# The graph part of an expert layer's tail: gathers in small portions behind the experts' steps

## The chip, the cores and the metric

The kernel runs on one core of a Trainium2 chip. The metric is the device time of one execution in microseconds (us), the median of several runs. A profile is one more execution, taken by the hardware profiler.

## The reference, cut to what matters

The input is `x` of shape (4, 32, 96, 256), which is 12,288 tokens of 256 features. Layer 0 is a pair of Mamba scans over the two axes. Layer 1 is additive attention (`tanh` of all query and key pairs), and then an expert layer whose gates come from a graph attention. Only that last part is touched:

```python
h = (x_flat @ W_gat).reshape(M, HEADS, NUM_EXPERTS)          # 4 heads, 4 experts
a_src = (h * att_src).sum(-1);  a_dst = (h * att_dst).sum(-1)
e = leaky_relu(a_src[src] + a_dst[dst], negative_slope=0.2)   # random edges and one loop per token
ee = exp(e - e_max[dst]);  alpha = ee / segment_sum(ee, dst)[dst]
agg = segment_sum(h[src] * alpha, dst)
scores = layernorm(agg).reshape(M, HEADS, NUM_EXPERTS).mean(1)
topk_s, topk_i = top_k(scores, 2);  w = softmax(topk_s)
for ei in range(4):
    g = where(topk_i == ei, w, 0).sum(-1)
    out = out + g * (gelu(x @ W1[ei] + b1[ei]) @ W2[ei] + b2[ei])
```

The result is `out` plus the layer's input. The 1,048,576 edges have ends in a wider range than there are tokens. Indices beyond the tokens clip to the last one, so most edges are of a kind that is only counted; the rest, at most 108 columns of 128 edges for each quarter of the tokens, are gathered one by one.

## The kernel before, in words

Everything ahead of the tail is the same in both kernels. The tail (`tail()`, with the class `Graph` for the edges and the class `Experts`) does two things side by side, step by step, in one Python loop that lays out every engine's instructions in order.

**Experts.** There are 24 blocks of 512 tokens and 4 experts. A unit is one expert on one block, and takes 3 steps. 37 units are left for the tail: the last expert of blocks 6 to 16, two of block 17, and all four of blocks 18 to 23; the others were done earlier, beside the attention. A unit's hidden part is 16 matmuls `ph` (L1629) with Gelu on ScalarE (`h`, L1711); its output part, one unit later, is 32 matmuls `po` (L1637), with a bias added on VectorE (`ko`, L1701, or `o`, L1704). Where the gates of a block's quarter are not known yet when the block's turn comes, its outputs are kept: they are stored to DRAM (`kept`), and later, once the gates are there, loaded again (`all`, 2 MB) and added up with the gates onto the layer's input `y` (0.5 MB), 16 VectorE instructions (`y<-all,gates,y`, L1714) and a store of 0.5 MB to a block. Blocks 0 to 18 are kept, blocks 19 to 23 are gated at once (`y<-o,gates,y`).

**Edges.** A quarter's 108 columns are 9 portions of 12 columns (`GP`), called m in the loop. The quarters go in the order 3, 2, 0, 1. A portion passes through four operations:

- `gather`: 12 indirect DMAs `gs<-tab_s` (L1338), issued by GpSimd (POOL), bring the source rows; in quarter 3 alone 12 more, `gd<-tab_a` (L1045), bring the destination rows. The other quarters' `gd` were fetched during the attention. `gs` has four buffers.
- `scores`: five small VectorE instructions (L1352 to L1356), the exponential on ScalarE (L1282) and a product on VectorE (`v`, L1283).
- `spread`: for each of three groups of 4 columns (`GG`), VectorE makes one-hot tiles `ol` and `oh` (L1371) and the product `rh` (L1375).
- `place`: TensorE adds a group up into PSUM by 8 matmuls `pa` (L1385; 4 columns, two instructions each).

After a quarter's 9 portions `finish` makes its gates in five parts. `ready[q]` is the step from which a quarter's gates count as known.

In the tail's loop, what belongs to the edges stands in a list `todo` by steps: it is issued at the start of a step, ahead of that step's matmuls. Portion m has its scores at step 10 + 3m, its gathers all at once ten steps earlier, its three groups in the following steps, one to a step. So `ready` is 44, 71, 98 and 125, while the experts end at step 114. A kept block is due after its `ready`, at least 4 steps after the last such block; the loop runs to step 149.

The first own-edge line for each token (`own_edges`, L1303 to L1330) and `topa`, an all-reduce on POOL, are at the loop's start; the first portion's gathers are issued ahead of `topa`.

The kernel already has a pacing of another kind in the attention stage: there a gather is held back by a one-element copy on POOL (`mark<-th`, L689) of a value that ScalarE has just made.

Of the kernel before, what the change touches and what calls it, by code (L numbers as in the profile page):

```python
# [17 lines left out]
F32 = mybir.dt.float32  # L18
# [3 lines left out]
AF = mybir.ActivationFunctionType  # L22
ALU = mybir.AluOpType
# [3 lines left out]
P = 128  # L27
# [3 lines left out]
NT = TOK // P  # L31
# [18 lines left out]
JB = 512  # L50
# [9 lines left out]
G1, K1 = 8, 4  # L60
GP, GG = 12, 4
EDGE_US = 2.3
G0, PART = 10, 6
QUARTERS = 3, 2, 0, 1
KO_BUFS = 2
SLOT_US, PRODUCT_US = 1.2, 0.11
# [955 lines left out]
class Edges:  # L1022
# [19 lines left out]
    def gather(self, q, c):  # L1042
        if (q, c) not in self.have:
            self.have.add((q, c))
            self.nc.gpsimd.indirect_dma_start(  # L1045
                out=self.gd[:, q, c, :], out_offset=None,
                in_=self.tab_a[q].rearrange("p n f -> (p n) f"),
                in_offset=bass.IndirectOffsetOnAxis(ap=self.di[:, q, c:c + 1], axis=0))
# [203 lines left out]
class Graph:  # L1252
# [4 lines left out]
    def __init__(self, ctx, tc, a, ed, tab_s, tab_a, gates):  # L1257
        self.nc, self.ed = tc.nc, ed
        self.tab_s, self.tab_a, self.gates = tab_s, tab_a, gates
        pool = lambda name, bufs, **k: ctx.enter_context(tc.tile_pool(name=name, bufs=bufs, **k))  # L1260
        self.const, self.wk = pool("gc", 1), pool("gw", 2)
        self.ps = pool("gp", 2, space=PSUM)
        self.bg, self.lg, self.lb = (self.load(a, k, HF) for k in ("bg_rep", "lg_rep", "lb_rep"))
        self.eps = self.new("eps2", [P, 1])
        self.nc.vector.memset(self.eps, 1e-5)
        self.got, self.parts = {}, 4 * CQ // GP

    def new(self, name, shape):
        return self.const.tile(shape, F32, tag=name, name=name)
# [59 lines left out]
        nc.vector.tensor_tensor(wl, wl, ed.cnt.unsqueeze(2).to_broadcast([P, NH, ROW]), ALU.mult)  # L1329
        nc.vector.tensor_tensor(acc, acc, wl, ALU.add)  # L1330

    def gather(self, j):
        nc, ed = self.nc, self.ed
        gs = self.wk.tile([P, GP, ROW], F32, tag="gs", name="gs", bufs=4)
        q, c0 = divmod(j * GP, CQ)
        rows = self.tab_s.rearrange("p n f -> (p n) f")
        for u in range(GP):
            nc.gpsimd.indirect_dma_start(  # L1338
                out=gs[:, u, :], out_offset=None, in_=rows,
                in_offset=bass.IndirectOffsetOnAxis(ap=ed.si[:, q, c0 + u:c0 + u + 1], axis=0))  # L1340
            ed.gather(q, c0 + u)
        self.got[j] = gs

    def scores(self, j):
        nc = self.nc
        gs = self.got.pop(j)
        q, c0 = divmod(j * GP, CQ)
        gd = self.ed.gd[:, q, c0:c0 + GP, :]
        e = self.wk.tile([P, GP, HEADS], F32, tag="e", name="e")
        sh = self.wk.tile([P, GP, HEADS], F32, tag="sh", name="sh")  # L1350
        v = self.wk.tile([P, GP, ROW], F32, tag="v", name="v")
        nc.vector.tensor_tensor(e, gs[:, :, 0:HEADS], gd, ALU.add)  # L1352
        self.leaky(e)
        nc.vector.tensor_tensor(sh, gd, self.topa.unsqueeze(1).to_broadcast([P, GP, HEADS]), ALU.add)
        self.leaky(sh)
        nc.vector.tensor_tensor(e, e, sh, ALU.subtract)  # L1356
        self.weighted(e, v, gs[:, :, HEADS:], GP)
        self.v = v

    def spread(self, j, g):  # L1360

        nc, ed = self.nc, self.ed
        q, c0 = divmod(j * GP + g * GG, CQ)
        cols = slice(c0, c0 + GG)
        ol = self.wk.tile([P, GG, P], F32, tag="ol", name="ol")
        oh = self.wk.tile([P, GG, NT], F32, tag="oh", name="oh")
        rh = self.wk.tile([P, GG, NT, ROW], F32, tag="rh", name="rh")
        for to, among, which in ((ol, ed.lanes, ed.lane),
                                 (oh, ed.tiles[:, q * NT:(q + 1) * NT], ed.tile)):
            n = to.shape[2]  # L1370
            nc.vector.tensor_tensor(to, among.unsqueeze(1).to_broadcast([P, GG, n]),  # L1371
                                    which[:, q, cols].unsqueeze(2).to_broadcast([P, GG, n]),
                                    ALU.is_equal)
        v = self.v[:, g * GG:(g + 1) * GG, :]
        nc.vector.tensor_tensor(rh, oh.unsqueeze(3).to_broadcast([P, GG, NT, ROW]),  # L1375
                                v.unsqueeze(2).to_broadcast([P, GG, NT, ROW]), ALU.mult)
        return ol, rh

    def place(self, j, g, ol, rh):
        nc = self.nc  # L1380
        c0 = (j * GP + g * GG) % CQ
        if c0 == 0:
            self.pa = self.ps.tile([P, JB], F32, tag="pa", name="pa")
        for u in range(GG):
            nc.tensor.matmul(self.pa[:, :NT * ROW], ol[:, u, :],  # L1385
                             rh[:, u].rearrange("p n f -> p (n f)"),
                             start=(c0 + u == 0), stop=(c0 + u == CQ - 1))

    def finish(self, q):

        nc = self.nc
        cols = slice(q * NT, (q + 1) * NT)
        new = lambda name, shape: self.wk.tile(shape, F32, tag=name, name=name, bufs=1)
        acc, gates = self.acc[:, cols, :], self.gates[:, cols, :]
        nc.vector.tensor_tensor(acc, acc, self.pa[:, :NT * ROW].rearrange("p (n f) -> p n f", f=ROW),
                                ALU.add)
        yield from gates_of(nc, new, acc, gates, self.bg, self.lg, self.lb, self.eps)

# [328 lines left out]
def tail(tc, a, ed, ex, w, tab_s, tab_a, gates):  # L1727


    with ExitStack() as ctx:  # L1730
# [3 lines left out]
        units = [(i, e) for i in range(NBLK_X) for e in range(NEXP) if (i, e) not in ex.done]  # L1734
        todo = {}

        def at(t, f):
            todo.setdefault(t, []).append(f)

        own = gr.own_edges()  # L1740
        for n in range(3):
            at(2 * n, lambda: next(own, None))
        hot, ready = {}, {}
        PQ = CQ // GP
        for m in range(4 * PQ):
            j = QUARTERS[m // PQ] * PQ + m % PQ
            t = G0 + PART * m // 2
            if m < 1:
                gr.gather(j)
            else:  # L1750
                at(max(0, t - 10), lambda j=j: gr.gather(j))
            at(t, lambda j=j: gr.scores(j))
            for g in range(GP // GG):
                at(t + 1 + g, lambda j=j, g=g: hot.update({(j, g): gr.spread(j, g)}))
                at(t + 2 + g, lambda j=j, g=g: gr.place(j, g, *hot.pop((j, g))))
            if m % PQ == PQ - 1:
                fin, q = {}, QUARTERS[m // PQ]
                t += 2 + GP // GG
                at(t, lambda q=q, fin=fin: fin.update(g=gr.finish(q)))
                for n in range(5):  # L1760
                    at(t + n, lambda fin=fin: next(fin["g"], None))
                ready[q] = t + 5

        gr.tables()

# [5 lines left out]
        for i in sorted(kept, key=due.get):  # L1771
            v = {}

            def fetch(i=i, v=v):
                v["o"], v["y"] = ex.outputs_tile(), ex.sums(i, "y2")
                tc.nc.sync.dma_start(v["o"], ex.kept[i])

            def half(q0, i=i, v=v):
                for q in (q0, q0 + 1):
                    for e in range(NEXP):  # L1780
                        ex.add(i, e, q, v["y"], v["o"][:, q, e, :])
                if q0:
                    ex.store(i, v["y"])

            t = free = max(free + 4, due[i] + 1)
            at(t - 4, fetch)
            at(t, lambda half=half: half(0))
            at(t + 2, lambda half=half: half(2))

        to, hs = {}, {}  # L1790
        end = max(todo) + 1
        for t in range(max(3 * len(units) + 3, end)):
            n, part = divmod(t, 3)
            for f in todo.get(t, []):
                f()
            if n < len(units):
                i, e = units[n]
                if part == 0:
                    ex.fetch(i)
                    hs[n] = ex.hp.tile([P, FC, TB], F32, tag="h1", name="h1")  # L1800
                    if i in kept:
                        to[n] = ex.place()
                    else:
                        to[n] = ex.sums(i) if first[i] == n else to[n - 1]
                if part == 1 and n + 1 < len(units):
                    ex.fetch(units[n + 1][0])
                for f in ((0, 1), (2,), (3,))[part]:
                    ex.gelu(i, e, f, hs[n])
            if n and n - 1 < len(units) and part:
                i, e = units[n - 1]  # L1810
                ex.outputs(i, e, hs[n - 1], 2 * (part - 1), to[n - 1], i not in kept)
                if part == 2:
                    if i in kept:
                        ex.keep(i, e, to[n - 1])
                    elif last[i] == n - 1:
                        ex.store(i, to[n - 1])
# [267 lines left out]
```

## Time and profile before

| | us |
|---|---|
| Median of 3 runs | 15,269.78 (15,255.12 to 15,275.91) |
| Profiled execution | 15,342.51 |
| its span | 15,340.7, granted TensorE clock 0.891 |
| First expert matmul of the tail's loop | 14,239.9 |
| Last use of an expert's result (`y<-o`, L1714) | 15,229.8 |
| Last matmul | 15,258 |

The tail's work lies from about 14,200 us to the end of the span. In the page, "slices" are the span in 40 equal parts of 384 us with the busy tenths of each engine; PE is TensorE's matmul, PEld its weight loads, DVE VectorE, ACT ScalarE, POOL GpSimd. The "chain of waits" follows the work that ended last back from the end, each piece with its start and length. A "group" takes the instructions of one line and form together: busy us, mean ns of one, then the idle time of its engine just ahead of them, and what ended it. "Windows" give busy time and (in brackets) the number of instructions of each engine in a stretch.

### The profile page before, as it was taken

To read this page: it belongs to the slowest core of one execution; us is meant where nothing else is said; L and a number is where in the kernel's file an instruction comes from. 1 tells how busy PE (TensorE), PEld (TensorE's weight loads), DVE (VectorE), ACT (ScalarE), POOL (GpSimd) and SP (SyncE) were. 2 spreads that over 40 slices of the span, in tenths; PEclk is the share of its full clock that TensorE was granted. 3 is DMA by queue.
4 is the path that set the end of the run, shared out by engine and by line. 5 is a ranking of instruction groups with operands and counts; after the bars stand their busy time and mean duration, and the time that the engine had idled before them with its cause. 6 is when DMAs were issued, how large, how long until landed. Compare 5 with 4: busy or idle time off the path is not lost.

```text
span 15340.7 us, 224408 instructions
## 1 busy us (share of the span) xinstructions
PE 11721.4 (76%) x86496; PEld 5149.6 (34%) x86496; DVE 10713.9 (70%) x15462; ACT 12165.7 (79%) x9327; POOL 8797.1 (57%) x6727
## 2 busy tenths in 40 slices
PE   5666665777777767888887777788877888888797
PEld 2222232222222233333333333333333344433454
DVE  7888888777777887777777877577777733312368
ACT  3444334999999979999999899999997899999121
POOL 4655556777777767767777677477650144100663
PEclk8888887888888888899999889999988999999898
DMA  5666665445545454455554444355541000000223
GB/s 191 204 203 202 199 203 166 147 149 155 151 151 149 157 155 148 150 153 151 149 152 156 151 148 152 108 152 151 151 129 43 16 15 10 24 25 22 51 62 128
DMA packets 1197836, 1986.91 MB, mean 130 GB/s; under 512 B 411984, under 2 KB 645072, under 8 KB 1194320
## 3 DMA queue, kind: packets, MB, share of 16 engines
q1 hardware_dynamic: 1169104, 1967.10, 41.5%
q0 software_dynamic: 27648, 5.36, 0.7%
q8 instruction: 680, 11.14, 0.3%
q14 instruction: 404, 3.31, 0.1%
HBM read 1864.71 MB, written 107.35 MB: 129 GB/s over the span
## 4 chain that ended last, share of the span: by engine, by line
PE 23%; ACT 20%; DVE 7%; issue 4%; DMA 1%; POOL 1%; another core or an unknown queue 0%; SPq 0%; DVEq 0%; ACTq 0%; POOLq 0%
ACT th L823 14%; PE pe L796 9%; PE pv L902 3%; ACT dA L385 3%; PE pa L1385 2%; PE po L1637 2%; PE ph L1629 2%; DVE h L402 1%; ACT pr L886 1%; PE ptw L893 1%; PE ex L1554 1%; PE pz L459 1%; PE px L215 1%; DVE dB L393 1%
## 5 line engine op out<-in xcount | busy, mean ns | idle before, releaser
L823 ACT ACTIVATE th<-krep,qsel 128x3072 f32<-128x3072 f32 x3072 | 8666.9, 2847 | 380.4 <-PE pe L796 359.1
L796 PE MATMUL pe<-th,wa_blk 128*32 128x384 f32 x49152 | 5045.0, 539 | 1612.6 <-ACT pr L886 1382.7
L409 POOL TENSOR_TENSOR h<-h,bC 128x768 f32<-128x768 f32 x2048 | 3756.1, 1834 | 3012.2 <-DVE h L402 2638.5
L402 DVE TENSOR_TENSOR_SCAN h<-dA,dB 128x384 f32<-128x384 f32 x4096 | 3686.6, 941 | 1041.0 <-ACT dA L385 712.9
L796 PEld LDWEIGHTS pe<-th,wa_blk 128*32 128x32 f32 x49152 | 1458.9, 116 | 4171.2 <-issue 1967.3
L393 DVE TENSOR_TENSOR dB<-bB,dtu 128x768 f32<-128x768 f32 x2048 | 1942.3, 948 | 130.1 <-DMA bB<-bc 98.0
L385 ACT ACTIVATE dA<-dt,t_A 128x380 f32<-128x380 f32 x2048 | 1127.1, 571 | 897.9 <-DVE h L402 893.3
L385 ACT ACTIVATE dA<-dt,d_A 128x372 f32<-128x372 f32 x2048 | 1102.8, 562 | 606.0 <-DVE h L402 601.5
L428 PE MATMUL py<-h,ident 128*128 128x384 f32 x2176 | 990.7, 587 | 682.2 <-POOL h L409 681.3
L416 POOL TENSOR_TENSOR h<-h 128x768 f32<-128x768 f32 x752 | 1419.5, 1888 | 53.6
L902 PE MATMUL pv<-xn,pT 128*32 128x257 f32 x18432 | 1101.8, 387 | 131.4 <-DVE pT L895 130.8
L961 POOL TENSOR_SCALAR sf<-sel,f 128x32 f32<-128x32 f32 x384 | 146.0, 403 | 1584.0 <-ACT f L957 1480.9
L895 DVE COPY pT<-ptw 128x512 f32<-128x512 f32 (+1 forms) x768 | 419.3, 546 | 738.7 <-PE ptw L893 738.2
L428 PEld LDWEIGHTS py<-h,ident 128*128 128x128 f32 x2176 | 438.2, 219 | 1243.2 <-POOL h L409 1015.2
L418 POOL TENSOR_TENSOR y<-y,h 128x384 f32<-128x384 f32 x752 | 784.2, 1043 | 59.0
L902 PEld LDWEIGHTS pv<-xn,pT 128*32 128x32 f32 x18432 | 579.8, 111 | 707.7 <-DVE pT L895 257.0
L417 POOL TENSOR_TENSOR h<-h 128x384 f32<-128x384 f32 x752 | 782.0, 1040 | 59.0
L1338 POOL DMA_INDIRECT gs<-tab_s,si x432 | 496.6, 1149 | 324.7 <-DVE v L1283 171.2
L879 DVE TENSOR_REDUCE nb<-pe 128x1 f32<-128x768 f32 x384 | 362.2, 943 | 408.7 <-PE pe L796 408.6
L1711 ACT ACTIVATE h<-ph,b 128x512 f32<-128x512 f32 x148 | 101.2, 687 | 688.6 <-PE ph L1629 513.5
L904 DVE COPY pvs<-pv 128x257 f32<-128x257 f32 x384 | 160.6, 418 | 609.7 <-PE pv L902 608.2
L893 PE MATMUL ptw<-ident,pr 128*128 128x128 f32 x2304 | 475.5, 324 | 106.6 <-DVE pT L895 37.6
(276 smaller groups left out, 14969.7 us busy)
## 6 DMA issues: line engine op xcount, KB each, us to landing
bB<-bc SPq DMA_DIRECT2D x2048, 384.0 KB
bC<-bc SPq DMA_DIRECT2D x2048, 384.0 KB
all<-kept SPq DMA_DIRECT2D x19, 2048.0 KB
x<-x SPq DMA_DIRECT2D x144, 256.0 KB
x<-x SPq DMA_DIRECT2D x192, 128.0 KB
xt<-xn2T SPq DMA_DIRECT2D x41, 512.0 KB
kept<-ko SPq DMA_DIRECT2D x39, 512.0 KB
qsel<-xn2T SPq DMA_DIRECT2D x75, 256.0 KB
```

The lines of the kernel that those rows point to most:

```text
L385: nc.scalar.activation(inner(dA[:, :T]), inner(blk["dt"][:, e, :]), AF.Exp, scale=blk["w"]["A"][:, e, i + s:i + s + 1])
L393: nc.vector.tensor_tensor(dB, blk["bB"].pop(j), z["dtu"].unsqueeze(1).to_broadcast([P, SB, T]), ALU.mult)
L402: nc.vector.tensor_tensor_scan(h[:, s, :], z.pop(("dA", e, i + s))[:, :T], z["dB"][:, s, :], 0.0, ALU.mult, ALU.add)
L409: nc.gpsimd.tensor_tensor(h, h, blk["bC"].pop(j), ALU.mult)
L416: nc.gpsimd.tensor_tensor(h0, h0, h1, ALU.add)
L417: nc.gpsimd.tensor_tensor(h0[:, 0, :], h0[:, 0, :], h0[:, 1, :], ALU.add)
L418: nc.gpsimd.tensor_tensor(y[e], y[e], h0[:, 0, :], ALU.add)
L428: nc.tensor.matmul(z["py"], self.ident, h[:, s, :], start=(i == 0), stop=(i == DS - 1))
L796: nc.tensor.matmul(pe[q * QU:(q + 1) * QU, j, :KQ // 2], self.wa[:, k, :], th[:, c0:c0 + KQ // 2], start=(k == 0), stop=(k == NK - 1))
L823: nc.scalar.activation(th, s["krep"], AF.Tanh, bias=s["qsel"][:, col:col + 1])
L893: nc.tensor.transpose(pt[:, (i - i0) * P:(i - i0 + 1) * P], pr[:, i * P:(i + 1) * P], self.ident)
L902: nc.tensor.matmul(pv[q * QU:(q + 1) * QU, :C + 1], pT[:, i, q * QU:(q + 1) * QU], s["xn"][:, q * NK + i, :], start=(i == 0), stop=(i == N ...
```

## The change

The loop of the tail now counts half steps: one half stands before a step's hidden matmuls, one between them and the output matmuls. `HALVES` says how many half steps 12 columns take: 8 in quarter 3, where each column needs two gathers, 2.5 in the others.

- Gathers: a portion's columns are dealt out one by one over its half steps, from half step 0 to 139. Ahead of the gathers of each half step stands `pace()`: a one-element memset `mark` on VectorE, and a copy of it on POOL to `seen` (both with two buffers). As an engine works in order, POOL does not go on to these gathers before VectorE has come to this half step. There are 140 such pairs.
- Scores of a portion come two half steps after its last gather, the product `v` (now `values`, an operation of its own) one later, the groups from the fourth on, spread over the time that the portion has, at least half a half step apart, and `place` one half step after `spread`. `v` has four buffers instead of two, and the PSUM tile `pa` is kept by quarter, since two quarters may overlap.
- The five parts of `finish` are a step apart, as before; `ready` becomes 46, 56, 67 and 78.
- Kept blocks are due every 3 steps instead of 4, the second half of a block three half steps after the first. With the new `ready` blocks 12 to 17 come at steps 57 to 72, 18 at 75, 0 to 5 at 78 to 93, and 6 to 11 at 96 to 111, and the loop ends at step 114, with the experts.
- The first portion's gathers are no longer ahead of `topa`.

The diff, cut to its core:

```diff
-G0, PART = 10, 6
+HALVES = 2.5, 8.0
...
+    def pace(self):
+        mark, seen = (self.wk.tile([P, 1], F32, tag=k, name=k) for k in ("mark", "seen"))
+        self.nc.vector.memset(mark, 0.0)
+        self.nc.gpsimd.tensor_copy(seen[0:1, :], mark[0:1, :])
...
-        v = self.wk.tile([P, GP, ROW], F32, tag="v", name="v")
+        v = self.wk.tile([P, GP, ROW], F32, tag="v", name="v", bufs=4)
...
+        h = free = 0.0
         for m in range(4 * PQ):
...
-            t = G0 + PART * m // 2
-            if m < 1:
-                gr.gather(j)
-            else:
-                at(max(0, t - 10), lambda j=j: gr.gather(j))
-            at(t, lambda j=j: gr.scores(j))
+            wide = HALVES[q == B - 1]
+            for u in range(GP):
+                calls.setdefault(int(h + wide * u / GP), []).append((j, u))
+            h += wide
+            at(h + 2, lambda j=j: gr.scores(j))
+            at(h + 3, lambda j=j: gr.values(j))
-            for g in range(GP // GG):
-                at(t + 1 + g, lambda j=j, g=g: hot.update({(j, g): gr.spread(j, g)}))
-                at(t + 2 + g, lambda j=j, g=g: gr.place(j, g, *hot.pop((j, g))))
+            for g in range(PG):
+                free = max(h + 4 + g * wide / PG, free + 0.5)
+                at(free, lambda j=j, g=g: hot.update({(j, g): gr.spread(j, g)}))
+                at(free + 1, lambda j=j, g=g: gr.place(j, g, *hot.pop((j, g))))
             if m % PQ == PQ - 1:
...
-                t += 2 + GP // GG
-                at(t, lambda q=q, fin=fin: fin.update(g=gr.finish(q)))
+                fin, s = {}, int(free) + 2
+                at(s, lambda q=q, fin=fin: fin.update(g=gr.finish(q)))
                 for n in range(5):
-                    at(t + n, lambda fin=fin: next(fin["g"], None))
-                ready[q] = t + 5
+                    at(s + 2 * n, lambda fin=fin: next(fin["g"], None))
+                ready[q] = s // 2 + 5
+        def beside(half):
+            for f in todo.pop(half, []):
+                f()
+            if half in calls:
+                gr.pace()
+                for j, u in calls.pop(half):
+                    gr.gather(j, u)
...
-            t = free = max(free + 4, due[i] + 1)
-            at(t - 4, fetch)
-            at(t, lambda half=half: half(0))
-            at(t + 2, lambda half=half: half(2))
+            t = free = max(free + 3, due[i] + 1)
+            at(2 * t - 8, fetch)
+            at(2 * t, lambda half=half: half(0))
+            at(2 * t + 3, lambda half=half: half(2))
...
         for t in range(max(3 * len(units) + 3, end)):
             n, part = divmod(t, 3)
-            for f in todo.get(t, []):
-                f()
+            beside(2 * t)
...
                 for f in ((0, 1), (2,), (3,))[part]:
                     ex.gelu(i, e, f, hs[n])
+            beside(2 * t + 1)
             if n and n - 1 < len(units) and part:
```

More of the change, by code (lines that the diff above doesn't have):

```diff
@@ L1265, in __init__ @@
         self.nc.vector.memset(self.eps, 1e-5)
-        self.got, self.parts = {}, 4 * CQ // GP
+        self.got, self.v, self.pa = {}, {}, {}
     def new(self, name, shape):
@@ L1330, in own_edges, with gather @@
         nc.vector.tensor_tensor(acc, acc, wl, ALU.add)
-    def gather(self, j):
+    def pace(self):
+        mark, seen = (self.wk.tile([P, 1], F32, tag=k, name=k) for k in ("mark", "seen"))
+        self.nc.vector.memset(mark, 0.0)
+        self.nc.gpsimd.tensor_copy(seen[0:1, :], mark[0:1, :])
+    def gather(self, j, u):
         nc, ed = self.nc, self.ed
-        gs = self.wk.tile([P, GP, ROW], F32, tag="gs", name="gs", bufs=4)
+        if j not in self.got:
+            self.got[j] = self.wk.tile([P, GP, ROW], F32, tag="gs", name="gs", bufs=4)
         q, c0 = divmod(j * GP, CQ)
[L1336 to L1342, printed above, removed]
+        nc.gpsimd.indirect_dma_start(
+            out=self.got[j][:, u, :], out_offset=None, in_=self.tab_s.rearrange("p n f -> (p n) f"),
+            in_offset=bass.IndirectOffsetOnAxis(ap=ed.si[:, q, c0 + u:c0 + u + 1], axis=0))
+        ed.gather(q, c0 + u)
     def scores(self, j):
@@ L1356, in scores, with values @@
         nc.vector.tensor_tensor(e, e, sh, ALU.subtract)
-        self.weighted(e, v, gs[:, :, HEADS:], GP)
-        self.v = v
+        nc.scalar.activation(v[:, :, HF:], e, AF.Exp)
+        self.got[j], self.v[j] = gs, v
+    def values(self, j):
+        v = self.v[j]
+        self.nc.vector.tensor_tensor(
+            v[:, :, :HF].rearrange("p n (h x) -> p n h x", x=NEXP),
+            self.got.pop(j)[:, :, HEADS:].rearrange("p n (h x) -> p n h x", x=NEXP),
+            v[:, :, HF:].unsqueeze(3).to_broadcast([P, GP, HEADS, NEXP]), ALU.mult)
     def spread(self, j, g):
@@ L1373, in spread @@
                                     ALU.is_equal)
-        v = self.v[:, g * GG:(g + 1) * GG, :]
+        v = self.v[j][:, g * GG:(g + 1) * GG, :]
         nc.vector.tensor_tensor(rh, oh.unsqueeze(3).to_broadcast([P, GG, NT, ROW]),
@@ L1380, in place @@
         nc = self.nc
-        c0 = (j * GP + g * GG) % CQ
+        q, c0 = divmod(j * GP + g * GG, CQ)
         if c0 == 0:
-            self.pa = self.ps.tile([P, JB], F32, tag="pa", name="pa")
+            self.pa[q] = self.ps.tile([P, JB], F32, tag="pa", name="pa")
         for u in range(GG):
-            nc.tensor.matmul(self.pa[:, :NT * ROW], ol[:, u, :],
+            nc.tensor.matmul(self.pa[q][:, :NT * ROW], ol[:, u, :],
                              rh[:, u].rearrange("p n f -> p (n f)"),
@@ L1394, in finish @@
         acc, gates = self.acc[:, cols, :], self.gates[:, cols, :]
-        nc.vector.tensor_tensor(acc, acc, self.pa[:, :NT * ROW].rearrange("p (n f) -> p n f", f=ROW),
+        nc.vector.tensor_tensor(acc, acc, self.pa.pop(q)[:, :NT * ROW].rearrange("p (n f) -> p n f", f=ROW),
                                 ALU.add)
@@ L1735, in tail, with at @@
         todo = {}
-        def at(t, f):
-            todo.setdefault(t, []).append(f)
+        def at(half, f):
+            todo.setdefault(int(half), []).append(f)
         own = gr.own_edges()
         for n in range(3):
-            at(2 * n, lambda: next(own, None))
-        hot, ready = {}, {}
-        PQ = CQ // GP
+            at(4 * n, lambda: next(own, None))
+        ready, calls, hot = {}, {}, {}
+        PQ, PG = CQ // GP, GP // GG
+        h = free = 0.0
         for m in range(4 * PQ):
-            j = QUARTERS[m // PQ] * PQ + m % PQ
-            t = G0 + PART * m // 2
-            if m < 1:
-                gr.gather(j)
-            else:
-                at(max(0, t - 10), lambda j=j: gr.gather(j))
-            at(t, lambda j=j: gr.scores(j))
-            for g in range(GP // GG):
-                at(t + 1 + g, lambda j=j, g=g: hot.update({(j, g): gr.spread(j, g)}))
-                at(t + 2 + g, lambda j=j, g=g: gr.place(j, g, *hot.pop((j, g))))
+            q = QUARTERS[m // PQ]
+            j = q * PQ + m % PQ
+            wide = HALVES[q == B - 1]
[8 more added lines that the diff above has]
+                at(free + 1, lambda j=j, g=g: gr.place(j, g, *hot.pop((j, g))))
             if m % PQ == PQ - 1:
-                fin, q = {}, QUARTERS[m // PQ]
-                t += 2 + GP // GG
-                at(t, lambda q=q, fin=fin: fin.update(g=gr.finish(q)))
+                fin, s = {}, int(free) + 2
+                at(s, lambda q=q, fin=fin: fin.update(g=gr.finish(q)))
                 for n in range(5):
-                    at(t + n, lambda fin=fin: next(fin["g"], None))
-                ready[q] = t + 5
+                    at(s + 2 * n, lambda fin=fin: next(fin["g"], None))
[7 more added lines that the diff above has]
+                    gr.gather(j, u)
         gr.tables()
@@ L1783, in half @@
                     ex.store(i, v["y"])
-            t = free = max(free + 4, due[i] + 1)
-            at(t - 4, fetch)
-            at(t, lambda half=half: half(0))
-            at(t + 2, lambda half=half: half(2))
+            t = free = max(free + 3, due[i] + 1)
+            at(2 * t - 8, fetch)
+            at(2 * t, lambda half=half: half(0))
+            at(2 * t + 3, lambda half=half: half(2))
         to, hs = {}, {}
-        end = max(todo) + 1
+        end = max(todo) // 2 + 1
         for t in range(max(3 * len(units) + 3, end)):
             n, part = divmod(t, 3)
-            for f in todo.get(t, []):
-                f()
+            beside(2 * t)
             if n < len(units):
```

## The prediction

> **What bounds the kernel now.** I read the page's slices first, then the chain of waits of the tail (14,197 us to the end), then windows and groups by form, and last the rows of single gathers. The change leaves all before the tail as it was, so only the last three of the page's 40 slices (384 us each) count:
>
> ```profile
> PE   5666665777777767888887777788877888888797
> ...
> POOL 4655556777777767767777677477650144100663
> ```
> PE (7, 9, 7 tenths) is the busiest engine and is missing at both ends; POOL (6, 6, 3) is not full. The chain of waits tells where PE is missing:
>
> ```profile
> 14277.20 50.60 issue
> ...
> 14328.55 9.73 another core or an unknown queue
> ...
> 14340.61 39.68 another core or an unknown queue
> ...
> 14381.06 5.51 PE po L1637 x16
> ...
> 14406.55 3.45 PE po L1637 x16
> ...
> 14429.98 3.45 PE po L1637 x16
> ...
> 15286.90 3.46 DMA out<-y
> 15290.38 8.61 DMA y<-x
> ...
> 15314.86 4.17 DMA out<-y
> 15319.05 7.19 DMA y<-x
> ```
> From 14,277 to 14,381 the chain has no engine in it (the start stall). From 14,381 it is matmuls; 14,406.55 to 14,429.98 is one unit of three steps, 23.4 us. The last expert result is used at 15,229.8 (y, L1714); after it come the last scatter groups, the last quarter's gates, and six late kept blocks with their loads and stores: 111 us to 15,340.7 (the overhang). The windows say the same of both places:
>
> ```profile
> 14280.00:14340.00 60.00, 9.65 (x22) 5.34 (x20) 1.55 (x6) 2.36 (x3) 42.77 (x46) 0.60 0.11 14
> 14340.00:14400.00 60.00, 18.94 (x54) 11.52 (x55) 11.75 (x18) 8.06 (x11) 25.61 (x28) 0.63 0.10 20
> ...
> 14460.00:14520.00 60.00, 60.00 (x185) 34.87 (x184) 28.66 (x46) 15.98 (x20) 48.42 (x39) 1.00 0.22 41
> ...
> 15240.00:15300.00 60.00, 14.24 (x31) 5.95 (x29) 52.09 (x119) 1.88 (x3) 0.00 (x0) 0.65 0.51 182
> ```
> The columns are PE, PEld, DVE, ACT, POOL, granted PE clock, DMA share, GB/s. In the stall PE works 10 of 60 us while POOL gathers without pause; in the third row PE is full with POOL at 48; in the last DVE alone works.
>
> **Prices.** All work of the tail, 14,240 to the end, by form:
>
> ```profile
> L1338 POOL DMA_INDIRECT gs<-tab_s,si x420 | 485.0, 1155 | 299.4 <-DVE v L1283 171.2 <-issue 124.2 <-DMA gs<-tab_s,si 3.4
> L1385 PE MATMUL pa<-rh,ol 128*128 128x480 f32 x864 | 379.7, 584 | 44.8 <-DVE rh L1375 42.3 <-issue 2.5
> ...
> L1375 DVE TENSOR_TENSOR rh<-oh,v 128x1920 f32<-128x1920 f32 x108 | 233.1, 2159 | 5.5 <-remote 1.8
> ```
> A matmul's duration counts its pipeline; by the distance between starts in the chain, po costs 0.216 (3.45 for 16), ph 0.43, pa 0.402 (3.22 for 8). A unit of 16 ph and 32 po is 13.8, a step 4.6, a scatter group 3.22; 13.8 + 3 x 3.22 = 23.5 is the 23.4 above. Single rows price POOL:
>
> ```profile
> 14343.71 0.95 POOL L1338 DMA_INDIRECT gs<-tab_s,si  x1 [0.30 <-issue]
> ...
> 14404.06 2.06 POOL L1338 DMA_INDIRECT gs<-tab_s,si  x1 [0.30 <-issue]
> ...
> 13018.97 0.18 POOL L689 COPY mark<-th 1x1 f32<-1x1 f32 x1 [1.12 <-ACT th L823]
> 13019.62 0.97 POOL L1045 DMA_INDIRECT gd<-tab_a,di  x1 [0.48 <-issue]
> ```
> A gather is 0.95 + 0.30 = 1.25; one that meets a scatter group's DVE work is longer (here 2.06). Of runs without a pause, 213.0 us from 14,396 held 146 gathers and 27 groups: (213.0 - 146 x 1.25) / 27 = 1.1 a group; 81.5 us from 14,611 held 58 and 9: 1.0; shorter ones gave 0.8 to 0.9. The last two rows are the attention stage's pacing, a one-element copy ahead of a gather: 0.18 + 0.48 = 0.66 behind a wait, and 0.18 + 0.17 = 0.35 where there was none.
>
> The Trainium skill, "SBUF — State Buffer", section "Who interferes with whom", speaks against the change: a VectorE instruction with two SBUF inputs contends with a GpSimd one that reads SBUF, and the second to issue fully blocks. By that, an estimate: each of 103 groups blocks gathers for its 2.16 + 0.68 + 0.25 us, 318 us instead of my 98, and an end 220 later. The trace agrees on a slowdown and not on that size, since 1.1 is the most that a group added.
>
> **Part by part.**
> Gathers. Before, a whole m of 12 columns was issued at once, as early as four gs buffers let it, and from the second quarter on POOL had 3 steps (23.4 us) for 12 gathers. After, all 540 (324 single, 108 pairs) are spread over half steps 0 to 139, behind a pace each: 216 in quarter 3's 36 steps, 324 in the next 34. POOL for a step: quarter 3, 6 x 1.25 + 0.75 x 0.95 + 2 x 0.44 = 9.1, against PE's 4.6 + 0.75 x 3.22 = 7.0; later 9.6 x 1.25 + 2.4 x 0.95 + 0.9 = 15.2 against 12.3. POOL is the longer in both: it becomes the bound. Its sum: 540 x 1.25 = 675; 103 groups beside it x 0.95 = 98 (82 to 113 by 0.8 and 1.1); 140 paces x 0.44 = 62 (49 to 92; 0.44 because the attention stage's 324 copies and gathers took (329.2 + 151.6 + 66.2) / 324 = 1.69 each by their groups, 1.25 of it the gather). Together 835, 806 to 880.
>
> Its start. Before, the first gathers ran at 14,197; after, they stand behind the first mark, which follows the own-edge line L1324 on DVE (14,246.3) and the all-reduce on POOL. 14,247, or 14,229 if a short PE lag there (14,207 to 14,234), which also lies beside streaming gathers, goes. Last gather: 14,247 + 835 = 15,082 (15,035 to 15,127).
>
> The new wait. mark and seen have two buffers: DVE's memset n waits for POOL's copy n-2. Behind it on DVE queue the spreads (PE's pa), the o and ko evictions (which free po for PE) and the kept adds; so DVE, and through it PE, walks in step with POOL, which I have already made the bound. The other way, POOL's copy waits for a memset that stands behind that half step's DVE work: 1.2 groups x 3.1, an eviction 0.7, and in twelve halves half a kept block, 4.0: 8.4, plus scores 1.4, against POOL's 7.6. POOL loses 0 to 30 there, I take 15. The 140 memsets themselves cost DVE under 0.2 us each beside 50% idle: nothing; if that cover were gone, 28. values() split off and v with 4 buffers move the same instructions; SP issues the same DMAs, kept loads earlier; two more activation-table loads of 1.28 lie in ACT's idle time (18 of 60 us busy at most). All at nothing.
>
> After the last gather. Half step 139.5 leaves 41.7 steps of experts (192) and six groups (19), then one eviction, two adds, store and end, 9 by the rows after the last add before (6.4) plus 2.6: 220. The four quarters' gates are known at steps 46, 56, 67, 78, so the remaining twelve kept blocks, one every 3 steps (13.8 us), end with the experts at step 114. Their 3.4 MB each then ask 246 GB/s; before, two took some 20 us in the overhang, 300 GB/s, so they fit, and 8 of DVE in 13.8 fits too.
>
> Sum in the profiled execution: 15,082 + 15 + 220 = 15,317 against 15,340.7: the 111 of overhang and the 105 of stall go, and the experts end some 80 later than they did, because POOL holds them. Its ends: 15,255 to 15,377.
>
> To the runs shown: the profiled execution took 15,342.5, 72.7 above the median. Either that surplus sits in the stall (85 us in it without PE work, with no engine, load or instruction fetch late), and goes with it, or it is spread and stays. I take four fifths for the first: it is the only place where time goes with no cause that the trace names, and a unit's 23.4 elsewhere agrees with its matmuls. 15,317 + 2 (outside the span) - 15 = 15,304; I say 15,305 (15,257 to 15,364).
>
> **Rivals.**
> Faster. POOL is cheap (0.8, 0.35, start 14,229: 15,255 + 2) and the 72.7 is spread, so that both kernels shed it: 15,257 - 73 = 15,184; with the middle prices 15,319 - 73 = 15,246. Centre 15,215. For it: bursts behind one pace, no wait in POOL's steady runs. Against it: nothing in the windows between 14,400 and 14,580 looks stretched by profiling.
> Slower: PE starves. In the stall PE lost 85 us in which about 84 gathers streamed (105 / 1.25): 1 us a gather. If streaming gathers do that to PE whenever it is not running full, paced quarter 3 (6 a step) makes PE's step 7.0 + 6 = 13 against POOL's 9.1: up to 36 x 3.9 = 140, 15,445. It decides from (9.1 - 7.0) / 6 = 0.35 us a gather. For it: both lags lie beside streams. Against: from 14,396 POOL streamed and PE was full.
> The gates come early and the end does not: kept blocks wait for DMA beside the experts' own loads (xt, y), losing 1 to 3 us in each of the last twelve: 15,317 to 15,340.
>
> **How the numbers follow.** A measurement of this kernel tells about 0.2% (31 us) from no change: faster is under 15,239, slower over 15,300. POOL-bound sum: 0.50, of it same 0.24, slower 0.26. Faster rival: 0.25, nearly all faster (0.24). PE starving: 0.17, slower. DMA-bound end: 0.08, slower. So 0.24 faster, 0.25 same, 0.51 slower. The range 15,205 to 15,390 leaves out the lower third of the faster rival (0.08) and the upper part of the starving one (0.08), and little of the rest. The cases have both signs; the likeliest one's own range is 15,257 to 15,364.
>
> **What would show it.** Right: POOL nearly without idle other than 0.30 to 0.66 from 14,250 to about 15,080; PE at 75 to 85% with a clock below 1.00 (at 48.62 of 60 it was 0.89); the last gather near 15,082; mark on DVE waiting for seen; no stretch of 50 us without PE; the last expert store within 10 us of the end. Wrong: a last gather before 15,035 or after 15,127 (POOL's price), PE lags in quarter 3 (starving), an end over 15 us after the last expert (kept blocks), or a surplus over the median that is still 73.

## The result, and the profile after

The changed kernel takes 15,302.6 us (median of 9, 15,294.7 to 15,316.8); the kernel before, timed beside it, 15,268.8 (9 runs). The ratio is 1.0023, interval 1.0013 to 1.0033: 34 us slower, and 2 us from the 15,305 that was predicted.

A second profile of the kernel before (e6 below) has to be told first, because the one that the prediction was made from took 15,342.5, 62 us more than the slowest of these nine runs. The comparisons ran on different chips, and the chips differ here: in two of the comparisons (the first one and that of e5 to e8) before takes 15,257 to 15,269, in three others, each on a chip of its own, 15,316 to 15,321. Its profile from one of these three (e1) has the start stall that the prediction describes. So I cut every execution at the last L1011 (the end of the attention's projections), at the first and at the last gather behind it, and compare these pieces in us:

| execution | L1011 at | to the first gather | gathers, first to last | last gather to end | tail |
|---|---|---|---|---|---|
| before, first profile (stall) | 14,195.5 | 2.1 | 965.2 | 177.9 | 1145.2 |
| before, e1 (stall) | 14,170.1 | 2.1 | 965.6 | 177.6 | 1145.3 |
| before, e6 (no stall) | 14,165.7 | 2.1 | 910.8 | 176.4 | 1089.3 |
| changed, first profile | 14,170.7 | 32.3 | 843.6 | 247.5 | 1123.4 |
| changed, e5 | 14,179.4 | 32.3 | 846.3 | 247.2 | 1125.8 |

The 34 us can be read off rows three and four: gathers start 30 us later (they now stand behind `topa`, and in e2, which has no marks, they start 27.6 us after L1011 as well; the first mark adds the other 5), their stream is 67 us shorter, and 71 us more are left behind the last one. (Row five, from e6's own chip, gives 30, 64 and 71.)

The page's slices of the changed kernel:

```profile
PE   5667774777777767878887778788877888888888
...
POOL 4555556777777767767767677477650144100782
```

In the last three slices POOL now has 7, 8 and 2 tenths (6, 6 and 3 before) and PE 8 in each: it no longer falls off at the end. Its groups from the first gather to the last (columns: busy, mean ns of one, idle before and what ended it):

```profile
L1343 POOL DMA_INDIRECT gs<-tab_s,si x432 | 524.7, 1215 | 111.6 <-issue 111.6
L1045 POOL DMA_INDIRECT gd<-tab_a,di x108 | 123.6, 1144 | 32.9 <-issue 32.9
L1336 POOL COPY seen<-mark 1x1 f32<-1x1 f32 x139 | 50.1, 361 | 0.9 <-DVE mark L1335 0.2
```

All of POOL's idle time is "issue", the fixed gap ahead of an instruction; but for 0.9 us it waited for nobody. In the first profile of before, 171 us of its idle time were put down to `v`, a wait for a gs buffer. The stream is full, as predicted, and single rows of POOL show what a pace costs:

```profile
14216.53 0.94 POOL L1045 DMA_INDIRECT gd<-tab_a,di  x1 [0.30 <-issue]
14217.47 0.18 POOL L1336 COPY seen<-mark 1x1 f32<-1x1 f32 x1
14217.81 0.97 POOL L1343 DMA_INDIRECT gs<-tab_s,si  x1 [0.16 <-issue]
```

The copy follows the gather without a gap, and the gap behind it is 0.16 in place of 0.30: 0.18 + 0.16 - 0.30 = 0.04 us, where I had put 0.44. (The copies' mean of 361 ns is longer than 0.18; that is counted with the collisions below.)

The chain of waits near the end of the stream:

```profile
15045.63 2.48 DMA gs<-tab_s,si
15048.23 0.22 DVE e L1356
...
15131.38 1.72 PE ph L1641 x4
...
15145.23 1.72 PE ph L1641 x4
...
15275.22 0.70 DVE o L1716
```

The last gather lands, scores, groups and gates follow on VectorE (until about 15,117, with TensorE at two thirds: 47.5 of 71 us), and then TensorE sets the time again, a unit every 13.85 us. The windows (columns as before) show the three phases:

```profile
14280.00:14340.00 60.00, 54.05 (x154) 31.12 (x155) 20.82 (x41) 9.59 (x12) 49.12 (x57) 0.90 0.19 40
...
14880.00:14940.00 60.00, 47.31 (x117) 24.10 (x118) 48.34 (x92) 11.38 (x14) 50.30 (x44) 0.89 0.26 68
...
15120.00:15180.00 60.00, 60.00 (x208) 39.29 (x207) 43.56 (x92) 10.99 (x16) 0.00 (x0) 0.99 0.71 252
```

In the first two PE has 54 and 47 of 60 us while POOL stands at 49 to 50, which with its gaps is all that it can do. In the third PE is full, POOL has nothing left, and the kept blocks load at 252 GB/s beside it.

### The profile page after: what moved, and what is told of

It is laid out like the page before. It is cut to its first block, busy times and chain, and to the rows that moved or that the text cites. A ratio compares the mean times of both kernels' runs of the same rounds, so it can differ in the third digit from the quotient of the medians.

```text
span 15294.1 us, 224663 instructions
## 1 busy us (share of the span) xinstructions
PE 11757.8 (77%) x86496; PEld 5154.2 (34%) x86496; DVE 10716.8 (70%) x15602; ACT 12162.3 (80%) x9328; POOL 8871.1 (58%) x6867
## 5 line engine op out<-in xcount | busy, mean ns | idle before, releaser
L1045 POOL DMA_INDIRECT gd<-tab_a,di x432 | 451.6, 1045 | 185.1 <-issue 182.0
```

## The experiments

Each is an edit of one of the two kernels; a ratio is to the kernel before on the same chip.

**e1, before unchanged.**

> The kernel before, unchanged, profiled once more. Theory (the surplus of its first profile sits in the start stall, and ordinary executions have none): span 15,255 to 15,285, and the stretch from 14,240 to 14,400 has PE busy in most of every 60 us window, no piece of 50 us without an engine. Rival (the surplus is spread by profiling): a span near 15,340 again, with the stall of some 105 us in it.

Measured: 15,317.2, a span of 15,315.4; before's runs on this chip have a median of 15,316.6. Both theories miss. The stall is there, in an execution that is usual on this chip:

```profile
14260.00:14320.00 60.00, 9.67 (x20) 5.66 (x20) 1.91 (x7) 4.50 (x6) 45.03 (x48) 0.56 0.09 14
14320.00:14380.00 60.00, 24.57 (x70) 14.79 (x71) 15.00 (x21) 5.93 (x8) 23.55 (x24) 0.67 0.09 20
```

**e6, before unchanged, on another chip.**

> The kernel before once more, on the same chip, to see by its profile how long its part ahead of the tail and its tail are here, and by its rounds how far two timings of one kernel lie apart: 0.999 to 1.001.

Measured: 15,251.4, ratio 0.9999 (0.9990 to 1.0008). Its profile has no stall; about the same stretch, counted from L1011, is:

```profile
14240.00:14300.00 60.00, 60.00 (x193) 36.25 (x192) 28.19 (x42) 16.36 (x21) 48.12 (x40) 1.00 0.22 57
14300.00:14360.00 60.00, 49.70 (x144) 29.02 (x143) 22.31 (x34) 10.90 (x14) 47.46 (x42) 0.89 0.17 40
```

So the stall costs 1145.2 - 1089.3 = 56 us, within the 47 to 64 us that lie between the chips' medians.

The rows show what TensorE's neighbours wait for in the stall. In e1 the first four of twelve `ph` matmuls are recorded as done at 14,251.39, and their Gelu on ScalarE starts 46.7 us later; in e6 (last two rows) it follows within 0.1 us:

```profile
14249.51 5.31 PE L1629 MATMUL ph<-xt,w 128*128 128x512 f32 x12
...
14298.04 0.69 ACT L1711 ACTIVATE h<-ph,b 128x512 f32<-128x512 f32 x1 [48.62 <-remote]
...
14254.70 3.60 PE L1629 MATMUL ph<-xt,w 128*128 128x512 f32 x8
...
14256.68 0.69 ACT L1711 ACTIVATE h<-ph,b 128x512 f32<-128x512 f32 x1 [7.76 <-PE ph L1629]
```

I counted the Gelus of the tail (148 in each profile) that start over 0.5 us after both their matmuls' recorded end and ScalarE's previous instruction. The five profiles of the changed kernel's first run and of e5 to e8 have none, with pacing or without (e6). In the others the unpaced kernels (the first profile of before, e1, e2, e10) have 5 to 11, 102 to 147 us together, and the paced ones (e3, e4, e9, e11, e12) 2 to 10, 3 to 34 us together; all lie in the stretch of the gathers. So on some chips TensorE's results reach the other engines late while gathers run, and the first profile of before looks like one from such a chip. Whether the matmuls took longer than recorded, or only the word of their end was late, the rows do not tell.

**e2, no pacing.** The changed kernel, and gathers only in their places:

```diff
-                gr.pace()
```

> The changed kernel without the 140 memset and copy pairs; the gathers stand in the same order. Theory (POOL's stream of gathers, with what VectorE's work adds to it, sets the time): the stream shrinks by what a copy costs beyond the gap that it replaces, 140 x 0.04 = 6 us, and by the copies that were held up, at most 25; the end within 15,270 to 15,305. Rival (the lock-step sets it: VectorE waited 92 us for seen, and TensorE behind it): 15,210 or less.

Measured: 15,351.4, 1.0028 (1.0018 to 1.0038), on the chip of e1; its tail is 1173.6. Neither theory: without the pairs it did not get faster, and the start stall is back:

```profile
14260.00:14320.00 60.00, 17.05 (x37) 7.59 (x35) 4.87 (x10) 3.59 (x5) 45.68 (x48) 0.64 0.09 14
14320.00:14380.00 60.00, 9.16 (x25) 5.72 (x26) 3.62 (x4) 0.69 (x1) 45.68 (x48) 0.54 0.07 5
```

Pacing is what takes the stall away: with it, none of the changed kernel's three profiles has a window like these (the lowest has 32 us of PE in 60), and one of the three, e12, is from a chip where before takes as long as here. e3 and e4 below, paced and on e2's own chip, have only 30 and 3 us of late Gelus, e2 has 147 us of them. e2's tail is 50 us longer than that of the changed kernel's first profile and 34 longer than e12's; both comparisons are between chips.

**e5 and e12, the changed kernel on two more chips.**

> The changed kernel itself, timed on this chip beside the kernel before, which the first comparison did on another chip. In the profiles the changed kernel's tail (from the last line of the attention's projections, L1011, to the end) took 1123.4 us, that of before 1145.2 and 1145.3 (two profiles). If these are usual executions, the ratio here is 0.9985 (22 us less) and the 1.0023 of the first comparison is another chip's; if the start stall of before is not in its usual executions, the ratio is again 1.002 or more.

> The changed kernel once more, beside the run with four marks. If the chip is one on which before shows the start stall (its median over 15,300): 0.998 to 0.9995 of before, since the changed kernel's tail was 1123 to 1126 us and that of before with the stall 1145. If it is one without (before near 15,260, tail 1089): 1.002 to 1.003 again.

Measured: e5, on a chip where before takes 15,257.2 (e6's), 1.0026 (1.0016 to 1.0036); e12, where before takes 15,315.9, 1.0003 (0.9994 to 1.0012), with a tail of 1139.1. The sign of the first comparison is thus one of a chip without the stall; with it the two kernels are equal. e12 is 11 us above the upper end of its forecast (15,308). The changed kernel's own stream was 860 us there, 13 to 16 longer than in its other profiles, and its ten late Gelus (34 us together) lie in the same stretch.

**e4, without quarter 3's destination gathers** (its scores read another quarter's rows):

```diff
-        ed.gather(q, c0 + u)
+        if q != 3:
+            ed.gather(q, c0 + u)
...
-        gd = self.ed.gd[:, q, c0:c0 + GP, :]
+        gd = self.ed.gd[:, q % 3, c0:c0 + GP, :]
```

> The changed kernel without quarter 3's 108 destination gathers (its scores read another quarter's rows, so the result is not the reference's). Theory: POOL's stream is 135 us shorter; in quarter 3 TensorE's 7.0 us a step takes over from POOL's 9.1, so 36 x 2.1 = 76 us come off there, and the end is at 15,215 to 15,235. Rival (POOL is not the bound, it only looks full): less than 30 us.

Measured: 15,242.2 (one run), tail 1074.5: 49 to 51 us less than in the changed kernel's profiles without late results, and 65 less than e12's; between the two forecasts and nearer to the first. The gathers' stretch is 794.7, 49 shorter; in quarter 3 PE comes to the front:

```profile
14380.00:14440.00 60.00, 59.38 (x178) 33.98 (x178) 23.89 (x51) 13.07 (x17) 33.59 (x44) 0.98 0.27 84
```

POOL is the bound there with the 108 gathers in. Quarter 3, from its first source gather to that of the next quarter, takes 258.1 us in place of 312.5, or 7.2 us a step in place of 8.7. TensorE's 7.0 is thus nearly reached; that 54 us came off and not 76 is mostly because POOL's step had been 8.7 and not 9.1.

**e7, three half steps more between gathers and scores:**

```diff
-            at(h + 2, lambda j=j: gr.scores(j))
-            at(h + 3, lambda j=j: gr.values(j))
+            at(h + 5, lambda j=j: gr.scores(j))
+            at(h + 6, lambda j=j: gr.values(j))
...
-                free = max(h + 4 + g * wide / PG, free + 0.5)
+                free = max(h + 7 + g * wide / PG, free + 0.5)
```

> The changed kernel with scores, values and groups three half steps later behind their gathers (5, 6 and 7 in place of 2, 3 and 4), all else as it was. Theory (POOL's stream is full and sets the time until the last gather): within 10 us of the changed kernel. Rival (what sets it is the loop from a gather's landing through the scores, VectorE's work ahead of the next mark, and that mark back to POOL): at least 40 us less.

Measured: 15,279.1, 1.0015 (1.0006 to 1.0024), 18 us less than e5 on the same chip. The stream is as long as it was (842.7, e5 846.3); 11 of the gain lie behind the last gather. With a full stream the loop through the scores does not lengthen it: the theory's cause held, its bound of 10 did not quite.

**e3 and e8, the gathers dealt out more thinly.** e3 is the changed kernel with `HALVES = 4.0, 9.5`, e8 is e7 with `HALVES = 4.0, 9.0`.

> The changed kernel with HALVES 4.0 and 9.5 in place of 2.5 and 8.0: the same gathers, groups and paces, dealt out over 97 steps of the experts in place of 70; the gates are known at step 106 in place of 78. Theory: the gather stream is as long as it was (it is POOL's own time, some 840 us), so the last gather stays within 20 us of 15,045, and 17 steps of experts are left behind it in place of 42: 15,060 + 78 + 19, and the last six kept blocks at some 10 us each after gates at 15,100: 15,150 to 15,190. Rival (a half step has a length of its own, by waits between scores, landing and the marks): 54 half steps more at the 6 us that they took come back, and the end is at 15,300 or later.

> HALVES 4.0 and 9.0 with the same three half steps more. With 4.0 and 9.5 alone the gather stream was no longer full (POOL waited 180 us for marks) and the end did not move. If the loop through the scores held it there, the added slack frees it: the last gather at 840 to 870 us after the first, the end some 120 us behind it, 130 to 170 us less than the changed kernel. If something else holds it (the one-step waits between spread, the matmuls and the evictions, or VectorE's own order), less than 40.

Measured: e3 15,331.7, 1.0008 (0.9999 to 1.0017); e8 15,294.8, 1.0028 (1.0017 to 1.0039), on e5's chip and 2.5 us from e5. My theory fell twice. In e3 the gathers take 974 us, in e8 939, and now POOL waits (engine, what for, us in total, times, longest; e3):

```profile
POOL seen L1336 <- DVE mark L1335: 180.0, 41, 11.2
```

The chain of e3 shows the loop:

```profile
14918.18 0.48 DVE y L1726
...
14918.75 0.56 POOL seen L1336
...
14919.48 0.97 POOL gs L1343
...
14925.57 2.15 DMA gs<-tab_s,si
14927.73 0.20 DVE e L1356
```

The mark stands behind a kept block's adds, POOL's gathers of that half step behind the mark, the scores behind their landing, and VectorE's next mark behind the scores. e8 takes the landing out of this loop (the three half steps), yet marks remain: POOL waited 127 us for them, VectorE 80 us for `seen`, in turn.

**e9 and e11, more marks.** e8 with the scores 8 half steps behind (values 9, groups 10) and

```diff
-        mark, seen = (self.wk.tile([P, 1], F32, tag=k, name=k) for k in ("mark", "seen"))
+        mark, seen = (self.wk.tile([P, 1], F32, tag=k, name=k, bufs=8) for k in ("mark", "seen"))
```

e11 has `bufs=4`.

> HALVES 4.0 and 9.0, scores, values and groups eight, nine and ten half steps behind their gathers, and eight buffers in place of two for mark and seen, so that VectorE need not wait for POOL until it is eight half steps ahead. In the run with 4.0, 9.0 and three half steps more, POOL waited 127 us for marks and VectorE 80 us for seen in turn. Theory (two marks tie VectorE and POOL together, and TensorE to both, so that none can make up for another's slow half steps): with eight, the gather stream fills again, its last gather 830 to 870 us after the first (there 936), and the end comes 80 to 120 us before that run's; 0.993 to 0.997 of before on a chip where before has no start stall. Rival (the tie is between spread, matmuls and evictions, one half step apart, on VectorE's own queue): within 25 us of that run, 1.001 or more.

> The run with eight marks, with four. With eight, TensorE did 20.0 us of work in the 60 us from 14,220, where POOL ran on through the first marks without a wait; from 14,280 it did 53 of 60. Theory (gathers that run on far ahead of VectorE hold TensorE up at the start, as in the start stall of before): four marks shorten that stretch to under 20 us of loss, and the tail from 1085.7 us to 1060 to 1075. Rival (the lull at the start has nothing to do with how far POOL is let ahead): the lull stays within 10 us, and with less room for VectorE the tail is 1085 or more.

Measured: e9 15,264.6, 0.9963 (0.9949 to 0.9976); e11 15,257.6, 0.9961 (0.9948 to 0.9975), both on chips where before takes 15,316 to 15,321 (e10 shows the stall on e9's), e11 beside e12: 61 us less than the changed kernel. The tails are 1085.7 and 1089.2, the gathers take 886.5 and 890.5 (e8 939). POOL's waits for marks fall from e8's 127 us to 65 and 64, VectorE's for `seen` from 80 to 2 and 15. e9's tail is 45 us shorter than e8's and not 80 to 120; but e9 has three half steps more for the scores as well, and another chip, so how much of the 45 is due to the marks is not shown. The lull at the start (first row e9, second e11):

```profile
14220.00:14280.00 60.00, 20.01 (x47) 11.05 (x46) 5.81 (x19) 5.17 (x7) 43.75 (x57) 0.66 0.11 22
```

```profile
14220.00:14280.00 60.00, 32.38 (x85) 19.70 (x86) 7.42 (x26) 6.83 (x9) 43.72 (x58) 0.72 0.14 31
```

Four marks win back 12 us of PE there, as the theory has it, but the tail is no shorter, as the rival has it; on the time of the tail the pair is inconclusive. The late results speak for the theory: the longest wait of VectorE for a `po` that is recorded as done is 32.0 us with eight marks, 19.8 with four, at most 9.9 with two (e3, e4, e12), and 84 without (e2). e11 is the version that beats both kernels, where before takes 15,316. Where before takes 15,260, e11 was not run; its tail there can be put beside the 1089.3 of e6 only as an argument, and by that it would be level with before.

**e10, before with even portions, unpaced** (and `v` and `pa` kept as in the change):

```diff
-            t = G0 + PART * m // 2
+            t = G0 + 4 * min(m, PQ) + 2 * max(0, m - PQ)
...
-            t = free = max(free + 4, due[i] + 1)
+            t = free = max(free + 3, due[i] + 1)
```

> The kernel before, without any pacing, with the portions 4 steps apart in quarter 3 and 2 in the others (3 throughout before), kept blocks every 3 steps, and v and pa kept by portion and quarter as the change does. The gates are known at step 108 or so, in place of 125 (and of 78 in the change). Theory (what counts is how much of TensorE's work is left behind the last gather: 230 us in the change, almost none with over 100 us of other work behind it in before): the gather stream and TensorE's 857 us end together, and the end is 40 to 90 us before that of before, 0.994 to 0.997. Rival (the order of before is bound by what each portion waits for, not by where POOL's and TensorE's work lie): within 15 us of before.

Measured: 15,301.1, 0.9988 (0.9979 to 0.9997), tail 1135.9, last matmul 54 us ahead of the end (before 81 to 82). A gain of 20, a third of the forecast's middle and 5 beyond the rival's; its profile has the start stall, of two windows in which PE did 28 of 120 us.

## Why the prediction was right, by its steps

**POOL becomes the bound: held.** The stream is full, e4 shortens the end by taking gathers out, and e7 leaves the stream as long as it was. From L1011 the prediction's sum reads 51.5 to the first gather (14,247), 835 + 15 of stream, 220 behind it: 1121.5. Measured 32.3, 843.6, 247.5: 1123.4. The total is right to 2 us, and its terms are not: that is luck.

**Its terms.** Gathers 540 x 1.25 = 675 as predicted. Paces: 6 us (140 x 0.04) in place of 62, and POOL waited 0.2 us for marks within the stream, not 15; the attention's row stood behind a wait, this copy takes the place of a gap. Collisions: the gathers' busy time is 648.3 against 540 x 0.95 = 513, 135 more, and copies 25 above 139 x 0.18: 160 us, 1.5 for each of the 104 groups in the stream, not 0.95. A gather beside a group's VectorE instructions took 1.56 us on average, one beside none 0.95, and the other VectorE work adds only 0.06; in e6, where POOL pauses and 95 groups lie in the stream, the excess of the gathers is 624.3 - 513 = 111. The paces' error and the collisions' cancel. The estimate by full blocking, from the Trainium skill's "SBUF — State Buffer", "Who interferes with whom" (318 us), is twice the 160 that was measured.

**The start, 19 us early:** I took 14,247 from a row of before, where `topa` stands behind the first portion's gathers, and behind the lag at 14,207. In the change it stands ahead of these gathers: L1324 comes 31 us after L1011, in place of 51, and of 45 in e6, which has no lag. I had kept 14,229 as the lower end only.

**Behind the last gather, 27 us late.** The price of experts and groups held (units of 13.85), but the last portion's scores, groups and gates left TensorE idle for 23.5 us until 15,117, which I had put at nothing, and the end has a kept half block between the last two evictions (the units and groups themselves took 6 us less than priced):

```profile
15275.22 0.69 DVE L1716 TENSOR_TENSOR o<-po,b 128x512 f32<-128x512 f32 x1 [2.83 <-PE po L1649]
15275.95 0.88 DVE L1726 SCALAR_TENSOR_TENSOR y<-o,gates,y 128x256 f32<-128x256 f32 x2
15276.75 7.92 DVE L1726 SCALAR_TENSOR_TENSOR y<-all,gates,y 128x256 f32<-128x256 f32 x16
15284.58 0.68 DVE L1716 TENSOR_TENSOR o<-po,b 128x512 f32<-128x512 f32 x1
```

I had 9 us for the end; it is 19 from 15,275.

**The surplus of 72.7.** I put four fifths of it into the start stall. Against e6 the first profile was 85.7 longer: 55.9 in the stall, 29.8 ahead of the tail. The 15 us that I took off as "spread" thus stand for those 25 to 30 that the changed kernel's profile, too, did not have ahead of its tail; why that part was longer stays open. (The 15 came off the upper end of 15,257 to 15,364 and not off the lower, which should have been 15,242.) I had read no engine as late in the stall; by the rows of e1 and e6 it is TensorE's results that are late. Profiling as such is no cause: e6 was profiled too and has no stall. That the chip decides is an inference from five profiles without late results and nine with them.

**The new wait** between mark and seen took 91.6 us of VectorE's time as forecast, without a price while POOL is full; when it is not, the marks stand in the chain that holds the tail (e3), and e8 has the same waits.

**The rivals.** "PE starves" under paced gathers did not occur; unpaced it did (e2). "The surplus is spread" fell with e1 and e6. The kept blocks were no bound: the last units run at 13.85 us with 252 GB/s beside them.

## What to carry to other kernels

Before work of one queue is pulled forward, add up that queue's own time: here POOL's 840 us and TensorE's 857 (37 x 13.8 + 108 x 3.22) are nearly equal, and packing the first into 70 of 114 steps leaves 247 us, most of them TensorE's, behind it. Gates that are known at step 78 of 114 are worth nothing if the engine that makes the end has been slowed to get them. Two engines that pace each other with two tokens pay for each other's slow steps once neither is full (e3, e8); four or eight tokens, with the work dealt out more thinly and more slack for the scores, took 61 us off the changed kernel on one chip, and which of the three did it is not separated.

## What the runs showed of the hardware that was not expected

A one-element copy between two gathers costs 0.04 us where VectorE does not disturb it, since it takes the place of most of the gap (0.30) between them. And on some chips, not on all, TensorE's results reach ScalarE and VectorE late while gathers run on unchecked at the tail's start, by up to 50.7 us in before and 84 in e2: 56 us of before's tail, with PE at 9 to 25 of 60 us. With two marks the longest such wait is 10 us, with four 20, with eight 32. Why a stream of gathers does that there, while a full and paced one later does so little, and why only on some chips, stays open.
